# Scaling a PSUM tile by halves, third product one pair later instead of two, first loads on a second queue: pairwise bilinear products on one core

## Chip, cores, metric

One core of a Trainium2 chip. The time is the device time of one execution in microseconds, a median of several runs. One core runs, so there is no die to compare.

In the lines of the profile PE is TensorE's matmuls, PEld its weight loads, ACT ScalarE, DVE VectorE, POOL GpSimd and SP SyncE, whose queue issues most transfers. A line of a page gives, after the bar, the busy time in us and the mean ns of one instruction, then the idle time of the engine just before and what ended it. PSUM is the memory into which TensorE writes its products.

## The reference, cut to what matters

```python
FIELD_SIZE, EMBED_SIZE = 32, 128                 # batch 1024, 496 pairs i < j
v_i, v_j = inputs[:, I_IDX, :], inputs[:, J_IDX, :]
transformed = jnp.einsum('bpd,ped->bpe', v_i, W)  # one 128x128 matrix a pair
return transformed * v_j                          # (1024, 496, 128), 260 MB of fp32
```

## The kernel before

All but the first 15 pairs split x and W into a high and a low part, so that three products of a faster kind (a matmul starts every 0.23 us, a native fp32 one every 0.43) are precise enough for the output check. A pair's PSUM tile is 128 partitions by 1024 fp32, two banks (the prediction says from where), and PSUM holds four such tiles. For each pair:

```python
# F: first product, high*high and low*low, two halves of the batch each
for t in (0, 1):
    for h in range(0, BT, HB):                    # HB = 512, one bank
        nc.tensor.matmul(po[q][:, h : h + HB], w_s[c][t][:, r], x_s[i][t][:, h : h + HB],
                         start=t == 0, stop=t == 1)
nc.scalar.mul(po[q], po[q], 1.0 + EPS)            # A: the whole tile, in place
...
if q >= LAG:                                      # LAG = 2
    if q - LAG >= nq0:
        second(q - LAG)                           # S: third product, two matmuls into the same tile
    finish(q - LAG)                               # D: times x_j on VectorE, then store 512 KB
```

[...] Weights come in chunks of four pairs; ScalarE and GpSimd split each chunk two chunks ahead. What builds the instruction lists from the program (called the compiler here) is free to reorder the instructions of an engine; F, A, S and D are used as names below, with F0, F1, A0, A1 for the half of the batch.

Of the kernel before, what the change touches and what calls it, by code (L numbers as in the profile page):

```python
# [1 line left out]

# [4 lines left out]

F32 = mybir.dt.float32
F32R = mybir.dt.float32r
ALU = mybir.AluOpType  # L10

P = 128
NF = 32
NQ = NF * (NF - 1) // 2
BT = 1024
HB = 512
WC = 4
EPS = 2.0**-12
NATIVE = 5
LAG = 2  # L20


def _pairs():

    return [(i, j) for i in range(NF - 2, -1, -1) for j in range(i + 1, NF)]


@with_exitstack
def kernel(
    ctx: ExitStack,  # L30
    tc: tile.TileContext,
    xt: bass.AP,
    wt: bass.AP,
    out: bass.AP,
):
















    nc = tc.nc
    pairs = _pairs()
    nchunk = NQ // WC

    xpool = ctx.enter_context(tc.tile_pool(name="x", bufs=1))
    spool = ctx.enter_context(tc.tile_pool(name="xs", bufs=2))
    rpool = ctx.enter_context(tc.tile_pool(name="wr", bufs=4))
    wpool = ctx.enter_context(tc.tile_pool(name="ws", bufs=3))
    tpool = ctx.enter_context(tc.tile_pool(name="tmp", bufs=2))  # L60
    opool = ctx.enter_context(tc.tile_pool(name="o", bufs=6))
    ppool = ctx.enter_context(tc.tile_pool(name="ps", bufs=4, space=bass.MemoryType.PSUM))

    x_sb = {}

    def load_x(f, pieces=1):
        x_sb[f] = xpool.tile([P, BT], F32, tag=f"x{f}", name=f"x_{f}")
        s = BT // pieces
        for k in range(pieces):
            nc.sync.dma_start(out=x_sb[f][:, k * s : (k + 1) * s], in_=xt[:, f, k * s : (k + 1) * s])  # L70

    w_raw = {}

    def load_w(c, splits=(0, WC)):
        w_raw[c] = rpool.tile([P, WC, P], F32, tag="w", name=f"w_{c}")
        for a, b in zip(splits, splits[1:]):
            nc.sync.dma_start(out=w_raw[c][:, a:b, :], in_=wt[:, c * WC + a : c * WC + b, :])

    w_s = {}

    def split_w(c):

        raw = w_raw[c].rearrange("p q e -> p (q e)")
        h, l, d = [wpool.tile([P, WC * P], F32R, tag=t, name=f"{t}_{c}") for t in ("wh", "wl", "wd")]
        hs = tpool.tile([P, WC * P], F32, tag="t", name=f"whs_{c}")
        nc.scalar.mul(h, raw, 1.0 - 2.0**-13)  # L86
        nc.gpsimd.tensor_tensor(l, raw, h.bitcast(F32), ALU.subtract)  # L87
        nc.gpsimd.tensor_scalar(hs, h.bitcast(F32), EPS, 1.0, ALU.mult, ALU.mult)  # L88
        nc.gpsimd.tensor_tensor(d, l.bitcast(F32), hs, ALU.subtract)  # L89
        w_s[c] = (h, l, d)  # L90

    x_s = {}

    def split_x(f):

        h, l, d = [spool.tile([P, BT], F32R, tag=t, name=f"{t}_{f}") for t in ("xh", "xl", "xd")]
        for a in range(0, BT, HB):
            s = slice(a, a + HB)
            ls = tpool.tile([P, HB], F32, tag="t", name=f"xls_{f}_{a}")
            nc.scalar.mul(h[:, s], x_sb[f][:, s], 1.0 - 2.0**-13)  # L100
            nc.gpsimd.tensor_tensor(ls, x_sb[f][:, s], h[:, s].bitcast(F32), ALU.subtract)  # L101
            nc.gpsimd.tensor_scalar(l[:, s], ls, 1.0 / EPS, 1.0, ALU.mult, ALU.mult)  # L102
            nc.gpsimd.tensor_tensor(d[:, s], h[:, s].bitcast(F32), l[:, s].bitcast(F32), ALU.subtract)  # L103
        x_s[f] = (h, l, d)

    nq0 = NATIVE * (NATIVE + 1) // 2
    c0 = nq0 // WC

    load_w(0, (0, 1, WC))
    load_x(NF - 2, 2)  # L110
    load_x(NF - 1, 2)
    load_x(NF - 3)
    load_w(1)
    for f in (NF - 4, NF - 5):
        load_x(f)
    load_w(2)

    out_v = out.rearrange("q e b -> q e b")
    po = {}

    def finish(q):
        j = pairs[q][1]
        ot = opool.tile([P, BT], F32, tag="ot", name=f"ot_{q}")
        pieces = 2 if q >= NQ - 2 else 1
        s0 = BT // pieces
        for k in range(pieces):
            s = slice(k * s0, (k + 1) * s0)
            nc.vector.tensor_tensor(ot[:, s], po[q][:, s], x_sb[j][:, s], ALU.mult)  # L128
            nc.sync.dma_start(out=out_v[q, :, s], in_=ot[:, s])

    def second(q):
        i, _ = pairs[q]
        r = slice(q % WC * P, (q % WC + 1) * P)
        for h in range(0, BT, HB):
            nc.tensor.matmul(  # L135
                po[q][:, h : h + HB], w_s[q // WC][2][:, r], x_s[i][2][:, h : h + HB], start=False, stop=True,
                skip_group_check=True,
            )

    for q in range(NQ + LAG):  # L140
        if q < NQ:
            i, j = pairs[q]
            c = q // WC
            if q % WC == 0:
                if c + 3 < nchunk:
                    load_w(c + 3)
                for k in ([c + 2] if c > 0 else [0, 1, 2]):
                    if c0 <= k < nchunk:
                        split_w(k)
            if j == i + 1:  # L150
                for f in ([i - 4] if i < NF - 2 else [NF - 6]):
                    if f >= 0:
                        load_x(f)
                if 0 <= i - 1 < NF - 1 - NATIVE:
                    split_x(i - 1)
            po[q] = ppool.tile([P, BT], F32, tag="po", name=f"po_{q}")
            if q < nq0:
                for h in range(0, BT, HB):
                    nc.tensor.matmul(  # L159
                        po[q][:, h : h + HB],  # L160
                        w_raw[c][:, q % WC, :],
                        x_sb[i][:, h : h + HB],
                        start=True,
                        stop=True,
                    )
            else:
                r = slice(q % WC * P, (q % WC + 1) * P)
                for t in (0, 1):
                    for h in range(0, BT, HB):
                        nc.tensor.matmul(  # L170
                            po[q][:, h : h + HB],
                            w_s[c][t][:, r],
                            x_s[i][t][:, h : h + HB],
                            start=t == 0,
                            stop=t == 1,
                        )
                nc.scalar.mul(po[q], po[q], 1.0 + EPS)  # L177
        if q >= LAG:
            if q - LAG >= nq0:
                second(q - LAG)  # L180
            finish(q - LAG)


# [25 lines left out]
```

## Time and profile before

| of the kernel before | |
|---|---|
| time, median | 898 us |
| span of the profiled run | 896.0 us |
| pace of the split pairs | 1.776 us a pair (from one S to the next, mean) |
| TensorE's own pace, six matmuls | 1.39 us |
| DMA queue, share of 16 engines | 92.3% |
| S with one other F between it and its own F | 356 of 481 |
| S right behind its own F | 125 of 481 |

The pace is well over what any engine needs for a pair; the difference is waiting. The last two rows say how the compiler ordered TensorE, counted from the start times in the trace. The lines themselves stand in the prediction.

### The profile page before, as it was taken

The page shows a single profiled execution, that of the slowest core. Times are in us where ns is not written, and L with a number is a line of the kernel's source. Part 1 is how long each engine was busy: PE and PEld are TensorE (multiplying, and loading weights), DVE is VectorE, ACT ScalarE, POOL GpSimd, SP SyncE. Part 2 cuts the span into 40 slices and gives each one's busy share as a digit, 9 for nine tenths or more (in the row PEclk, how much of TensorE's full clock was granted, in tenths as well). Part 3 has the DMA queues.
Part 4 walks back from the last instruction along what each step waited for, and adds up shares of the span by engine and source line. Part 5 has one row for each costly group of instructions (what it writes and reads, how often), then busy time and mean ns, then how long its engine had stood idle before and what let it go on. Part 6 is the DMA issues. An engine that isn't in the chain of part 4 may idle for free.

```text
span 896.0 us, 10407 instructions
## 1 busy us (share of the span) xinstructions
PE 761.1 (85%) x2946; PEld 526.2 (59%) x2946; DVE 607.0 (68%) x498; ACT 558.2 (62%) x655; POOL 549.5 (61%) x523
## 2 busy tenths in 40 slices
PE   7988888888888888888888888888888888898887
PEld 2455555555666565555565666655656566665665
DVE  3666666666777666676676767776667777677766
ACT  2266666666676566566665667665756666666565
POOL 1878877777666774664747565665655647474441
PEclk9999999999999999999999999999999999999999
DMA  8999999899999898998998999998998899999997
GB/s 329 416 340 370 360 355 343 318 361 338 376 357 362 332 370 327 339 361 320 353 343 336 343 363 356 355 352 321 355 341 334 336 339 330 343 345 339 337 342 304
DMA packets 94666, 310.03 MB, mean 346 GB/s; under 512 B 10513, under 2 KB 10769, under 8 KB 94609
## 3 DMA queue, kind: packets, MB, share of 16 engines
q1 hardware_dynamic: 94608, 309.37, 92.3%
q8 instruction: 23, 0.38, 0.2%
q14 instruction: 35, 0.28, 0.1%
HBM read 49.28 MB, written 260.05 MB: 345 GB/s over the span
## 4 chain that ended last, share of the span: by engine, by line
PE 32%; ACT 25%; issue 19%; POOL 11%; DMA 1%; DVE 0%; POOLq 0%; ACTq 0%; DVEq 0%
ACT po L177 20%; PE po L170 17%; PE po L135 14%; ACT wh L86 4%; POOL wl L87 4%; POOL wd L89 4%; POOL whs L88 2%; DMA out_dram<-ot 1%; ACT xh L100 1%; POOL xls L101 1%; DVE ot L128 0%; POOL xl L102 0%; POOLq L87 0%; ACTq L177 0%; POOL xd L103 0%
## 5 line engine op out<-in xcount | busy, mean ns | idle before, releaser
L128 DVE TENSOR_TENSOR ot<-po,x 128x1024 f32<-128x1024 f32 (+1 forms) x498 | 607.0, 1220 | 285.4 <-ACT po L177 141.7
L177 ACT ACTIVATE po<-po 128x1024 f32<-128x1024 f32 x481 | 476.9, 1009 | 298.5 <-PE po L170 298.5
L135 PE MATMUL po<-xd,wd 128*128 128x512 f32 x962 | 325.7, 420 | 123.8 <-ACT po L177 123.0
L87 POOL TENSOR_TENSOR wl<-w,wh 128x512 fp32r<-128x512 f32 x121 | 154.5, 1277 | 301.7 <-ACT wh L86 301.7
L135 PEld LDWEIGHTS po<-xd,wd 128*128 128x128 f32 x962 | 152.7, 188 | 257.5 <-ACT po L177 162.8
L170 PE MATMUL po<-xh,wh 128*128 128x512 f32 x962 | 300.9, 394 | 0.0
L170 PE MATMUL po<-xl,wl 128*128 128x512 f32 x962 | 298.1, 391 | 0.0
L170 PEld LDWEIGHTS po<-xl,wl 128*128 128x128 f32 x962 | 180.6, 188 | 42.2
L170 PEld LDWEIGHTS po<-xh,wh 128*128 128x128 f32 x962 | 180.6, 188 | 42.1 <-issue 0.5
L89 POOL TENSOR_TENSOR wd<-wl,whs 128x512 fp32r<-128x512 f32 x121 | 156.6, 1294 | 7.9
L86 ACT ACTIVATE wh<-w 128x512 fp32r<-128x512 f32 x121 | 75.5, 624 | 19.3 <-DMA w<-in_wt_dram 19.3
L88 POOL TENSOR_SCALAR whs<-wh 128x512 f32<-128x512 f32 x121 | 75.1, 621 | 10.2
L101 POOL TENSOR_TENSOR xls<-x,xh 128x512 f32<-128x512 f32 x52 | 67.4, 1296 | 4.2
L103 POOL TENSOR_TENSOR xd<-xh,xl 128x512 fp32r<-128x512 f32 x52 | 66.9, 1287 | 2.2
L100 ACT ACTIVATE xh<-x 128x512 fp32r<-128x512 f32 x52 | 32.1, 621 | 13.6 <-PE po L170 8.7
L102 POOL TENSOR_SCALAR xl<-xls 128x512 fp32r<-128x512 f32 x52 | 32.4, 623 | 4.4
L159 PE MATMUL po<-x,w 128*128 128x512 f32 x60 | 29.6, 656 | 6.2 <-DMA x<-in_xt_dram 6.2
L159 PEld LDWEIGHTS po<-x,w 128*128 128x128 f32 x60 | 12.3, 209 | 22.6 <-issue 21.6
L86 ACT ACT_TABLE_LOAD x1 | 1.3, 1283 | 0.7 <-PEq L196 0.7
L196 POOL MEMSET const-float32-0.0<- 128x1 f32 x1 | 0.1, 99 | 0.2 <-issue 0.2
L196 POOL MEMSET const-bfloat16-1.0<- 128x1 bf16 x1 | 0.1, 102 | 0.0
L196 POOL MEMSET const-uint8-127<- 128x1 uint8 x1 | 0.1, 102 | 0.0
(1 smaller groups left out, 0.1 us busy)
## 6 DMA issues: line engine op xcount, KB each, us to landing
out_dram<-ot SPq DMA_DIRECT2D x494, 512.0 KB, 3.8
w<-in_wt_dram SPq DMA_DIRECT2D x123, 256.0 KB, 3.9
x<-in_xt_dram SPq DMA_DIRECT2D x30, 512.0 KB, 6.0
x<-in_xt_dram SPq DMA_DIRECT2D x4, 256.0 KB, 4.4
out_dram<-ot SPq DMA_DIRECT2D x4, 256.0 KB, 2.6
w<-in_wt_dram SPq DMA_DIRECT2D x1, 192.0 KB, 2.6
w<-in_wt_dram SPq DMA_DIRECT2D x1, 64.0 KB, 1.8
```

The costliest lines, as they stand in the source:

```text
L86: nc.scalar.mul(h, raw, 1.0 - 2.0**-13)
L87: nc.gpsimd.tensor_tensor(l, raw, h.bitcast(F32), ALU.subtract)
L88: nc.gpsimd.tensor_scalar(hs, h.bitcast(F32), EPS, 1.0, ALU.mult, ALU.mult)
L89: nc.gpsimd.tensor_tensor(d, l.bitcast(F32), hs, ALU.subtract)
L100: nc.scalar.mul(h[:, s], x_sb[f][:, s], 1.0 - 2.0**-13)
L101: nc.gpsimd.tensor_tensor(ls, x_sb[f][:, s], h[:, s].bitcast(F32), ALU.subtract)
L103: nc.gpsimd.tensor_tensor(d[:, s], h[:, s].bitcast(F32), l[:, s].bitcast(F32), ALU.subtract)
L128: nc.vector.tensor_tensor(ot[:, s], po[q][:, s], x_sb[j][:, s], ALU.mult)
L135: nc.tensor.matmul(po[q][:, h : h + HB], w_s[q // WC][2][:, r], x_s[i][2][:, h : h + HB], start=False, stop=True, skip_group_check=True,)
L159: nc.tensor.matmul(po[q][:, h : h + HB], w_raw[c][:, q % WC, :], x_sb[i][:, h : h + HB], start=True, stop=True,)
L170: nc.tensor.matmul(po[q][:, h : h + HB], w_s[c][t][:, r], x_s[i][t][:, h : h + HB], start=t == 0, stop=t == 1,)
L177: nc.scalar.mul(po[q], po[q], 1.0 + EPS)
```

## The change

The intent: let A start after two of the four matmuls by working half by half, bring S close to its F, and save issue time at the start.

```diff
-LAG = 2
+LAG = 1
@@ (load_x takes the issuing engine)
-    load_x(NF - 2, 2)
-    load_x(NF - 1, 2)
+    load_x(NF - 2, 2, nc.scalar)
+    load_x(NF - 1, 2, nc.scalar)
@@ F and A
-                for t in (0, 1):
-                    for h in range(0, BT, HB):
+                for h in range(0, BT, HB):
+                    for t in (0, 1):
                         nc.tensor.matmul(
                             po[q][:, h : h + HB],
 [...]
-                nc.scalar.mul(po[q], po[q], 1.0 + EPS)
+                    nc.scalar.mul(po[q][:, h : h + HB], po[q][:, h : h + HB], 1.0 + EPS)
```

(A view of the output that did nothing was removed too.)

More of the change, by code (lines that the diff above doesn't have):

```diff
@@ L64, with load_x @@
     x_sb = {}
-    def load_x(f, pieces=1):
+    def load_x(f, pieces=1, eng=None):
         x_sb[f] = xpool.tile([P, BT], F32, tag=f"x{f}", name=f"x_{f}")
@@ L69, in load_x @@
         for k in range(pieces):
-            nc.sync.dma_start(out=x_sb[f][:, k * s : (k + 1) * s], in_=xt[:, f, k * s : (k + 1) * s])
+            (eng or nc.sync).dma_start(out=x_sb[f][:, k * s : (k + 1) * s], in_=xt[:, f, k * s : (k + 1) * s])
     w_raw = {}
@@ L116 @@
     load_w(2)
-    out_v = out.rearrange("q e b -> q e b")
     po = {}
@@ L128, in finish @@
             nc.vector.tensor_tensor(ot[:, s], po[q][:, s], x_sb[j][:, s], ALU.mult)
-            nc.sync.dma_start(out=out_v[q, :, s], in_=ot[:, s])
+            nc.sync.dma_start(out=out[q, :, s], in_=ot[:, s])
     def second(q):
```

## The prediction

> **What bounds the kernel now.** I read the page first (busy shares, then the idle column of the groups), then the table of stretches, then the waits, the timeline of one period, the chain of waits and last the tail. Short names: F is the first four matmuls of a pair (high and low halves, line 170), A is the activation that multiplies the pair's PSUM tile by 1+EPS (line 177), S is the third product (two matmuls, line 135), D is the VectorE multiply by the second field.
>
> ```profile
> PE 761.1 (85%) x2946; PEld 526.2 (59%) x2946; DVE 607.0 (68%) x498; ACT 558.2 (62%) x655; POOL 549.5 (61%) x523
> q1 hardware_dynamic: 94608, 309.37, 92.3%
> L177 ACT ACTIVATE po<-po 128x1024 f32<-128x1024 f32 x481 | 476.9, 1009 | 298.5 <-PE po L170 298.5
> L135 PE MATMUL po<-xd,wd 128*128 128x512 f32 x962 | 325.7, 420 | 123.8 <-ACT po L177 123.0
> L86 ACT ACTIVATE wh<-w 128x512 fp32r<-128x512 f32 x121 | 75.5, 624 | 19.3 <-DMA w<-in_wt_dram 19.3
> ```
>
> No compute engine is full. TensorE's 85% overstates it, because pipelined matmuls overlap in that count. What stands out is a pair that wait for each other: A waits 298.5 us for F, and S waits 123.0 us for A. That is a latency loop, not an engine at its limit. The other suspect is the DMA queue, whose packets fill 92.3% of 16 engines.
>
> One period of the steady state, TensorE alone (start, duration, what, idle before; the second half of the last two F is left out):
>
> ```profile
> 873.59 0.70 PE L135 MATMUL po<-xd,wd 128*128 128x512 f32 x2 [0.26 <-ACT po L177]
> 874.12 0.63 PE L170 MATMUL po<-xh,wh 128*128 128x512 f32 x2
> 874.59 0.62 PE L170 MATMUL po<-xl,wl 128*128 128x512 f32 x2
> 875.05 0.62 PE L135 MATMUL po<-xd,wd 128*128 128x512 f32 x2
> 875.51 0.63 PE L170 MATMUL po<-xh,wh 128*128 128x512 f32 x2
> 875.98 0.62 PE L170 MATMUL po<-xl,wl 128*128 128x512 f32 x2
> 876.43 0.63 PE L135 MATMUL po<-xd,wd 128*128 128x512 f32 x2
> 877.76 0.73 PE L135 MATMUL po<-xd,wd 128*128 128x512 f32 x2 [0.69 <-ACT po L177]
> 878.33 0.63 PE L170 MATMUL po<-xh,wh 128*128 128x512 f32 x2
> ...
> 879.26 0.62 PE L170 MATMUL po<-xh,wh 128*128 128x512 f32 x2
> ...
> 880.61 0.70 PE L135 MATMUL po<-xd,wd 128*128 128x512 f32 x2 [0.26 <-ACT po L177]
> ```
>
> The period is 880.61 - 873.59 = 7.02 us for four pairs (one weight chunk), 1.755 us a pair. A matmul starts every 0.233 us, so six take about 1.39 and four pairs 5.55. The missing 1.47 us lies at two places: an S that follows another S with nothing between (877.76), and an S after two F (880.61). The emitted order is thus not the program's order with LAG 2: never do three F stand ahead of an S. Counting over the trace, 356 of the 481 S have one other F between them and their own, and 125 have none, nearly always the last pair of a chunk. There the chain of waits shows why it is costly:
>
> ```profile
> 876.17 0.48 ACT wh L86
> 876.65 0.04 issue
> 876.69 1.03 ACT po L177
> 877.72 0.04 issue
> 877.76 0.73 PE po L135 x2
> ```
>
> The weight split (0.48 to 0.62 us on ScalarE) delays A, A is 1.0 us long and starts only when the whole F is done, and S waits for the whole A.
>
> In the tail, after the last weight split, S starts stand at 883.45 and 884.84: 1.39 us a pair, TensorE's own pace, even with today's A. So the loop is what holds the middle back.
>
> **What the Trainium skill says.** "ScalarE: Activation LUTs", What ACT_TABLE_LOAD costs: an activation with immediate scale and bias takes 186 ns + 0.833 ns an element, and neighbours overlap by 93 ns. Here 512 elements take 624 ns (612 by the formula) and 1024 in PSUM 1009 (1039): it agrees within 3%. "PSUM — Partial Sum Buffer", Specifications: a bank is 512 fp32 values a partition, so the tile is two banks and each half of the batch is a bank of its own; its section on bank collisions asks for guards by bank. The whole A straddles both, which is why it can't start after two matmuls. "DMA: Bandwidth & Descriptors", Issuing engines are not separate DMA queues: two issuers share the same 16 engines and only issue time is saved. The trace of before has one queue only and can't test it. "Perfetto Trace Analysis", Identifying the Most-Contended Engine, warns that matmul occupancy misjudges headroom; the tail's 1.39 us a pair against 1.755 agrees.
>
> **The change part by part.**
> 1. Scaling by halves with the matmuls reordered (half outside, term inside). Matmul count and weight loads stay (each of the four already has its own load). A becomes two of about 1009 - 512 x 0.833 = 582 ns, overlapping by 93: some 0.98 us of ScalarE a pair against 0.92. Cost 0.06 to 0.12 us x 481 = 30 to 60 us of ScalarE time, 1164 ns against 1009 in the busy column (+75 us), off the path: per chunk 4 x 0.98 + 0.53 + about 0.2 for the field split = 4.7 us, below TensorE's 5.55.
> Gain: the first half of A starts after two matmuls, not four. Today from F's start to its S there are 0.93 + 0.19 + 1.02 + 0.04 = 2.18 us. By halves the first half ends at 0.47 + 0.19 + 0.58 = 1.24, the second at about 1.72. So an S with nothing between stalls TensorE 1.28 - 0.93 = 0.35 us for the first half and about 0.25 more for the second, instead of 1.2; an S behind one F (2.32 us after its own F began, in strict alternation) has 0.6 us in hand, enough to swallow one weight split of 0.52.
> 2. LAG 1. It asks for the alternation F, S of the previous pair, which the order mostly has already. It removes nothing by itself; it takes the tendency to put two F together away. PSUM stays four tiles; in alternation a tile is used about 4.4 us and comes round after 5.55, so no wait for D appears.
> 3. First fields over the ScalarE queue. The first five field pieces cost 2.32 us of issue on the sync queue; x_30 can start about 0.9 us earlier, but x_29 and the next weights then share the engines with it. Native pairs end at 35.2 us now; I count 1 us gain, give or take 1.
>
> Sum for compute: a chunk of 5.55 plus 0.6 for one S without an F between = 6.2 us at most, 1.55 us a pair.
>
> **The DMA floor.** This is what will take over.
>
> ```profile
> 200.00:300.00 100.00, 85.36 (x340) 60.15 (x339) 69.47 (x57) 66.81 (x79) 68.91 (x65) 1.00 0.96 357
> ...
> 600.00:700.00 100.00, 84.86 (x337) 59.74 (x336) 68.40 (x57) 63.66 (x74) 60.55 (x58) 1.00 0.91 341
> 700.00:800.00 100.00, 86.95 (x347) 61.42 (x345) 70.72 (x59) 65.47 (x77) 58.63 (x57) 1.00 0.91 339
> ```
>
> The last two columns are DMA share and GB/s. From 200 to 800 us the share averages 0.925 and D's busy time over 1.22 us gives some 340 pairs, 1.766 us each. So a pair costs 1.766 x 0.925 = 1.63 us of all 16 engines, above the 1.55 of compute. Over the whole run: 92.3% of 896 is 827 us. In the stretch from 20 to 50 us the share reads 1.02 at 408 GB/s, so the engines can be filled. I take 97.5% filling, 1.63 / 0.975 = 1.675 us a pair, because reads of w among the writes will still make holes.
> Span: 34.2 to the end of the native pairs + 481 x 1.675 + 4 of tail = 844, and the measured times lie 2 above the span: **846 us**, 5.8% less.
>
> **Rivals.**
> (a) Order gone wrong: since each half is ready earlier, the compiler may place S right behind its own F always. Then F's start to the end of S is about 2.0 us a pair and the kernel is slower, about 1000 us. For it: it does so already in 125 of 481 places. Against: it does so where the next F has no PSUM tile yet. A milder form, the first half of S behind its own F and the second behind the next, costs 1.39 + 0.12 and stays under the DMA floor.
> (b) Only part of the loop gone: one stall of 0.6 a chunk stays and coincides with a hole in the DMA, so both add up: 6.2 + 0.7 = 6.9 us a chunk, 1.72 a pair, about 868 us.
> (c) DMA packets stretch less than I count. In quiet stretches a 4 KiB packet takes 159 ns, and the 827 us include those at 300 around the weight reads. If writes and reads interleave better, 1.55 to 1.6 a pair and 800 to 815 us.
> (d) ScalarE becomes the bound, by 75 us more of busy time: 633 of 845, 75%, no.
>
> **Range and chances.** The middle is the DMA floor with a little loss; the upper end is (b) with more order noise, the lower (c). 846, range 815 to 880. Faster by over 2% means under 880: 0.86. Within 2%: 0.10, if the order keeps most stalls. Slower: 0.04, rival (a).
>
> **What would show it.** S's wait for A falls from 123 us to under 50; A's group has 962 entries near 580 ns; PE starts alternate F and S at 1.5 to 1.7 us; the DMA share rises to 0.96 or more, D or SP start to wait for landings, and out's time from issue to landing grows from 3.8 us. It is wrong if the share stays at 0.92 with S waiting for A as before, or if S stand directly behind their own F throughout.

## The result, and the profile after

The changed kernel takes **1087.11 us** (median of 4 runs, 1086.47 to 1089.12) against 897.93. The ratio is 1.211 (95% interval 1.209 to 1.213).

The page of the changed kernel, the lines that answer to those of before (A is line 176 now, S 134, F 169):

```profile
PE 858.1 (79%) x2946; PEld 483.7 (44%) x2946; DVE 606.3 (56%) x498; ACT 616.2 (57%) x1136; POOL 548.3 (50%) x523
q1 hardware_dynamic: 94032, 308.32, 75.3%
L176 ACT ACTIVATE po<-po 128x512 f32<-128x512 f32 x962 | 524.6, 580 | 431.5 <-PE po L169 431.2
L134 PE MATMUL po<-xd,wd 128*128 128x512 f32 x962 | 356.5, 444 | 175.2 <-ACT po L176 174.9
L169 PE MATMUL po<-xh,wh 128*128 128x512 f32 x962 | 398.0, 414 | 45.4 <-ACT po L176 44.8
```

Every engine is less busy as a share, the DMA queue most of all (75.3% after 92.3%). The waits between F, A and S grew. The last line is new in kind: F, the pair's *first* product, now waits for ScalarE, 44.8 us, and its weight loads another 154.0 (list of waits). Before it never waited for A (0.0 us before both groups of line 170). What should F have to wait for in A? One period answers (all engines; start, duration, what, idle before):

```profile
603.86 0.39 PE L169 MATMUL po<-xh,wh 128*128 128x512 f32 x1
...
604.09 0.40 PE L169 MATMUL po<-xl,wl 128*128 128x512 f32 x1
604.12 1.07 ACT L176 ACTIVATE po<-po 128x512 f32<-128x512 f32 x2 [0.87 <-PE po L169]
...
604.75 0.73 PE L134 MATMUL po<-xd,wd 128*128 128x512 f32 x2 [0.27 <-ACT po L176]
...
605.24 0.19 PEld L169 LDWEIGHTS po<-xh,wh 128*128 128x128 f32 x1 [0.19 <-ACT po L176]
605.32 0.42 PE L169 MATMUL po<-xh,wh 128*128 128x512 f32 x1
```

603.86 and 604.09 are F0 of a pair; the two activations from 604.12 are A1 of the pair before and A0 of this pair, done at 605.19; then S of the pair before; and only at 605.24 come the weights of F1 of this pair, released by ScalarE. The compiled list of instructions says the same. An excerpt (TensorE, with the engine whose semaphore each instruction waits on; the words at the right are mine):

```
744 L134 Matmult po_2116<-xd_1684,wd_1982 128x512 [waits Activation]     S of the pair before
745 L134 Matmult po_2116<-xd_1684,wd_1982 128x512
746 L169 Matmult po_2128<-xh_1682,wh_1980 128x512 [waits Activation]     F1 of this pair
747 L169 Matmult po_2128<-xl_1683,wl_1981 128x512
748 L169 Matmult po_2140<-xh_1682,wh_1980 128x512 [waits DVE]            F0 of the next pair
749 L169 Matmult po_2140<-xl_1683,wl_1981 128x512
750 L134 Matmult po_2128<-xd_1684,wd_1982 128x512 [waits Activation]     S of this pair
```

(Numbers after the underscore name tiles.) F1 waits on ScalarE although it writes another bank than A0: the dependency is kept for the tile, not for its halves, and in the program A0 stands before F1. The same holds for S: its first matmul writes only the half that A0 scales, yet it waits for A1. Followed to the instruction that is waited for, the list has A0 of the same tile before F1, and A1 of the same tile before S, in all 481 pairs. The chain of waits of the changed kernel shows the loop that this makes:

```profile
604.12 0.59 ACT po L176
604.71 0.04 issue
604.75 0.73 PE po L134 x2
605.48 0.50 PE po L169 x2
...
606.07 0.59 ACT po L176
```

A1, then S of the same pair, then F1 of the next pair, then its A1: 1.95 us a pair, nothing beside it. The A0 that S's first half needs was done at 603.24, and S started at 604.75, right behind A1. F1 is held by two things that end within about 0.1 us of each other here, A0 (605.19) and the S that stands in front of it on TensorE; the chain goes through S. So this loop is the waits inside the tile together with the place of S between F0 and F1, and only the runs with a pinned order, below, tell the two apart. From F0's start of a pair (601.91, for the pair whose S starts at 604.75) to its S there are 2.84 us, against 2.18 in the kernel before and 1.28 in my prediction. From one S to the next a pair takes 2.180 us in the mean, where it was 1.776. In 393 of the 481 places half an F of the next pair lies between F and S, in 75 nothing.

One stretch, to be set beside the same stretch of the kernel before in the prediction:

```profile
600.00:700.00 100.00, 79.16 (x279) 45.18 (x277) 56.72 (x47) 58.03 (x108) 48.81 (x46) 1.00 0.77 288
```

279 matmuls in 100 us where there were 337; the DMA share falls from 0.91 to 0.77 because it has less to do.

### The profile page after: what moved, and what is told of

The parts are those of the page before. It is cut to its first block, busy times and chain, and to the rows that moved or that the text cites. A ratio compares the mean times of both kernels' runs of the same rounds, so it can differ in the third digit from the quotient of the medians.

```text
span 1087.1 us, 11362 instructions
## 1 busy us (share of the span) xinstructions
PE 858.1 (79%) x2946; PEld 483.7 (44%) x2946; DVE 606.3 (56%) x498; ACT 616.2 (57%) x1136; POOL 548.3 (50%) x523
## 3 DMA queue, kind: packets, MB, share of 16 engines
q1 hardware_dynamic: 94032, 308.32, 75.3%
## 4 chain that ended last, share of the span: by engine, by line
PE 57%; ACT 31%; issue 7%; POOL 2%; DMA 1%; ACTq 1%; DVE 1%; DVEq 0%; POOLq 0%
ACT po L176 30%; PE po L134 29%; PE po L169 27%; ACT xh L100 1%; PE po L158 1%; ACTq L176 1%; DMA w<-in_wt_dram 1%; DVE ot L127 1%; POOL xd L103 0%; POOL xls L101 0%; POOL wl L87 0%; ACT wh L86 0%; DMA x<-in_xt_dram 0%; POOL whs L88 0%; POOL xl L102 0%
## 5 line engine op out<-in xcount | busy, mean ns | idle before, releaser
L176 ACT ACTIVATE po<-po 128x512 f32<-128x512 f32 x962 | 524.6, 580 | 431.5 <-PE po L169 431.2
L134 PE MATMUL po<-xd,wd 128*128 128x512 f32 x962 | 356.5, 444 | 175.2 <-ACT po L176 174.9
L169 PE MATMUL po<-xh,wh 128*128 128x512 f32 x962 | 398.0, 414 | 45.4 <-ACT po L176 44.8
L169 PE MATMUL po<-xl,wl 128*128 128x512 f32 x962 | 379.3, 395 | 0.0
L134 PEld LDWEIGHTS po<-xd,wd 128*128 128x128 f32 x962 | 148.1, 188 | 378.2 <-ACT po L176 263.7
L169 PEld LDWEIGHTS po<-xh,wh 128*128 128x128 f32 x962 | 180.8, 188 | 179.3 <-ACT po L176 154.0
```

The costliest lines, as they stand in the source:

```text
L134: nc.tensor.matmul(po[q][:, h : h + HB], w_s[q // WC][2][:, r], x_s[i][2][:, h : h + HB], start=False, stop=True, skip_group_check=True,)
L176: nc.scalar.mul(po[q][:, h : h + HB], po[q][:, h : h + HB], 1.0 + EPS)
```

## The experiments

Every run but the last gave a correct result. Times are medians; the kernel before measured 896 to 898 us beside each.

**Which part of the change costs?** Each alone, and the queue. The theories that the expectations number are stated in the first of them, theory 4 where it comes up.

`lag1_only`: kernel before, `-LAG = 2` / `+LAG = 1`.

> The kernel before with LAG 1 instead of 2 and nothing else. Theory 1 (the loss is a wait inside one PSUM tile: the second half's matmuls F1 wait for the first half's activation A0 of the same tile) expects about the time of before, 880 to 910 us, since A is whole and there is no half to wait for. Theory 2 (LAG 1 puts the third product S too close behind its own first product) expects most of the loss here: 1000 us or more. Theory 3 (the doubled number of activations and their fixed cost) expects 898.

901.83 us, ratio 1.005 (1.002 to 1.008). The order on TensorE stays what it was: 354 S with one other F between, 127 with none. LAG 1 is not the cause.

`halves_only`: kernel before with only the F and A part of the diff.

> The kernel before, LAG 2 and one queue, with only the matmuls reordered by halves and A cut in two, as in the change. Theory 1 expects the whole loss here: 1070 to 1100 us, with F waiting for A some hundred times. Theory 2 expects no loss, 850 to 900 us. Theory 3 expects the loss here too, so it is told from theory 1 by the next run.

1083.13 us, ratio 1.2075 (1.204 to 1.211): all but 4 us of the loss, with LAG 2 and one queue.

`queue_only`: kernel before with only `+ nc.scalar` at the first field loads.

> The kernel before with only the four first field pieces issued on ScalarE's queue. All theories expect 898 within 4 us: some 1 us gained or lost before the native pairs.

894.77 us, ratio 0.9966 (0.9952 to 0.9980): 3 us gained, small but clear of noise. The start of its timeline:

```profile
0.73 1.85 ACTq L70 DMA_DIRECT2D x<-in_xt_dram  x4
...
3.87 12.45 PE L159 MATMUL po<-x,w 128*128 128x512 f32 x22 [3.87 <-DMA x<-in_xt_dram]
```

The field loads go out at 0.73 us instead of 1.65, the first matmul starts at 3.87 instead of 4.56, and the trace shows no gap in the first 22 matmuls, where the kernel before paused after four.

**Is it the wait of F1 for A0, or the halves themselves?**

`acts_last`: the changed kernel, activations written after all four matmuls.

```diff
                 for h in range(0, BT, HB):
                     for t in (0, 1):
                         nc.tensor.matmul(...)
+                for h in range(0, BT, HB):
                     nc.scalar.mul(po[q][:, h : h + HB], po[q][:, h : h + HB], 1.0 + EPS)
```

> The changed kernel with one edit: the two half activations are written after all four matmuls of the pair, so no matmul stands behind an activation of its own tile. The number and size of all instructions is that of the changed kernel. Theory 1 expects nearly all of the loss gone: 890 to 950 us (somewhat over before, since A0 and A1 one after the other end 0.15 to 0.2 us later than one whole A and this lies in the path about twice a chunk, 121 chunks). Theory 2 and theory 3 expect it to stay near 1087 us.

937.49 us, ratio 1.045 (1.042 to 1.048). The same instructions in number and size, LAG 1, and 150 us of the 189 lost are gone, so theories 2 and 3 are out as the main cause. In the compiled list 3 matmuls of F wait on ScalarE, all in the first pairs, where the changed kernel has 483.

`two_tiles`: the changed kernel with a PSUM tile per half.

```diff
-            po[q] = ppool.tile([P, BT], F32, tag="po", name=f"po_{q}")
+            po[q] = [ppool.tile([P, HB], F32, tag=f"po{g}", name=f"po{g}_{q}") for g in (0, 1)]
@@ finish
+        for k in (0, 1):       # D in two instructions of 512 columns, one store
```

> The changed kernel with a PSUM tile per half (512 columns, one bank, four of each half) in place of one tile of two banks; the multiply by the second field is then two instructions of 512 columns, about 0.69 us each. Theory 1 expects the wait of F for A to be gone and the gain that the halves were meant to bring to appear: 830 to 880 us, at a DMA share of 0.93 to 0.98. Theory 2 expects about 1087, since LAG is 1 here. Theory 3 expects about 1087 or more.

928.44 us, ratio 1.034 (1.032 to 1.037). F1 no longer waits for A0, and the result is right, so the chip doesn't need that wait: it came from the tile being one. But the gain I expected did not appear (928 against 830 to 880). The list of waits of this run shows where it went (waiting engine and line, releaser, us, times, longest):

```profile
PEld po L135 <- ACT po L177: 269.6, 700, 0.9
```

With the halves independent, the compiler put nearly every S (478 of 481) before the whole next F had been issued, its first half right behind F1 of its own pair, so the weight loads of S wait for A 700 times a little (195 times, 162.8 us, in the kernel before). My theory of the wait was right but not all: the order on TensorE is a second cause, and I took it to be at work in the kernel before as well, which the next runs test.

**The order on TensorE.** The pin used from here on keeps the instruction order only and adds no wait on the chip (TensorE's compiled list has 1236 semaphore waits in the kernel before and as many in the first run below):

```diff
-                        nc.tensor.matmul(            # F
+                        last[0] = nc.tensor.matmul(
@@
-                second(q - LAG)
+                with tc.issue_after(last[0].ins) if q < NQ else ExitStack():
+                    second(q - LAG)
```

`before_order`: kernel before, LAG 1, this pin.

> The kernel before with LAG 1 and whole activations, and the third product S of a pair pinned, in TensorE's issue order only, behind the first product F of the next pair (no semaphore is added). Theory 4 (what is left of the loop in the kernel before is the order on TensorE, S placed right behind its own F in 125 of 481 places and two F together elsewhere) expects the stalls to shrink to the one weight split a chunk, TensorE near 1.5 us a pair, and the DMA floor of 1.63 us a pair to take over: 845 us, 825 to 870. Its rival, that the order doesn't matter since A or the DMA hold the pace anyway, expects 890 to 905.

**781.54 us**, ratio 0.871 (0.869 to 0.872), better than my range. 480 of 481 S have just one other F between. Page and timeline of this run (A is line 178, S 136, F 171):

```profile
PE 732.3 (94%) x2946; PEld 526.8 (68%) x2946; DVE 606.7 (78%) x498; ACT 567.4 (73%) x655; POOL 550.4 (71%) x523
q1 hardware_dynamic: 94608, 309.37, 100.6%
L136 PE MATMUL po<-xd,wd 128*128 128x512 f32 x962 | 309.0, 402 | 3.3 <-ACT po L178 3.1
```

```profile
500.80 0.63 PE L136 MATMUL po<-xd,wd 128*128 128x512 f32 x2
501.27 0.62 PE L171 MATMUL po<-xh,wh 128*128 128x512 f32 x2
501.73 0.63 PE L171 MATMUL po<-xl,wl 128*128 128x512 f32 x2
502.19 0.62 PE L136 MATMUL po<-xd,wd 128*128 128x512 f32 x2
```

S, F, S, F at 1.39 us, and S waits for A 3.1 us in the whole run, where it was 123.0. The same work, one line of order: 902 (`lag1_only`) to 782 us.

`two_tiles_order`: `two_tiles` with the pin.

> A PSUM tile per half as in the earlier run, with S of a pair pinned behind the whole F of the next pair. The earlier run gave 928 us with its S halves one half product behind their own F. Theory 4 expects 845 us, 825 to 870, as TensorE and VectorE (two multiplies of 0.69 us) then both have about 1.4 us of work a pair. If instead the halves cost in themselves (more instructions, more semaphores), it stays over 900.

779.90 us, ratio 0.869 (0.867 to 0.871), again below my range: the halves on their own tiles cost nothing once the order is right, and gain nothing over whole activations either. (This kernel has the second queue too; the one with whole activations and that queue, at the end of this part, takes 778.4.)

`after_order`: the changed kernel with the pin.

> The changed kernel with the same pin of S behind the next pair's F, one PSUM tile of two banks as in the change. Theory 1 (F1 waits for A0 of its own tile) expects no cure: from F0's start to A0's end 1.24 us, then 0.04, F1 0.46, S 0.46, so about 2.2 us a pair and 1098 us, 1050 to 1120. If the order alone were what cost the changed kernel its time, 840 to 900.

1028.02 us, ratio 1.145 (1.143 to 1.147), 59 us better than unpinned and below my range: the pin left the compiler free to pull F0 of the pair after next forward, and it did so for 187 S. The wait stands plainly in TensorE's timeline:

```profile
600.82 0.39 PE L170 MATMUL po<-xh,wh 128*128 128x512 f32 x1
601.05 0.39 PE L170 MATMUL po<-xl,wl 128*128 128x512 f32 x1
602.11 0.50 PE L170 MATMUL po<-xh,wh 128*128 128x512 f32 x1 [0.67 <-ACT po L177]
```

F0 at 600.82 and 601.05, then F1 only at 602.11, when A0 (601.48 to 602.06 in the same run) is done.

`acts_last_order`: `acts_last` with the pin; it differs from `after_order` only in where the two activations stand.

> The changed kernel, one PSUM tile of two banks and two half activations, with S pinned behind the next pair's F, and the two activations written after all four matmuls. It differs from the pinned changed kernel (1028 us) only in where the two activations stand, so the difference is what the wait of F1 for A0 costs under a fixed order. Theory 1 expects 780 to 800 us: the two A end at 0.93 + 0.19 + 1.20 = 2.32 us after F began, S is due at 2.32, and the DMA sets 1.55 us a pair. If the halves themselves cost, it stays over 900.

814.57 us, ratio 0.908 (0.906 to 0.909). So under the pin the place of two activations is worth 213 us. It is 15 us over my range. A1 waits on A0 of its tile in the compiled list, so the two do not overlap:

```profile
499.92 1.20 ACT L178 ACTIVATE po<-po 128x512 f32<-128x512 f32 x2 [0.67 <-PE po L170]
```

1.20 us against 1.01 for one whole A. S is due 2.32 us after F began, just when the second activation ends, which leaves nothing in hand, and behind a weight split it waits (42.2 us in all for the matmuls, 137.8 for their weight loads). With a tile per half and the pin this cost is gone (779.9).

`before_order_lag2`: as `before_order`, LAG 2, so the order is that of the program before.

> The kernel before with LAG 2 and S pinned behind the F of two pairs later, which is what its program said. It tells what the LAG is worth where the order is kept. With four PSUM tiles, D of a pair (0.2 + 1.22 us) must end within the 1.39 us from its S to the F four pairs on, so TensorE waits a little for D in every pair: about 1.5 to 1.6 us a pair, 785 to 815 us. If it were 780 as with LAG 1, the LAG makes no difference; if near 898, the pin does not help by itself.

779.58 us, ratio 0.869 (0.867 to 0.870): no worse than LAG 1. I expected 5 to 35 us more from D holding PSUM tiles; at 1.52 us a pair there was time for it. So LAG is worth nothing either way, once the order is kept.

`before_order_queue`: `before_order` plus the second queue for the first fields.

> The kernel before with LAG 1, whole activations, S pinned behind the next pair's F, and the first field pieces on ScalarE's queue: the two parts that helped, together. If the gains add up, 3 us less than the pinned kernel: 778 us. If the DMA, full from start to end there, hides the earlier start, 781.

**778.43 us**, ratio 0.867 (0.866 to 0.869): 3 us under `before_order`, as much as the queue gave alone. That the gains add up is likely and not shown: the two ran in different rounds, and `before_order_lag2`, in the same rounds as this one and without the queue, is only 1 us slower. It takes 13.3% less time than the kernel before and its result is correct.

**What bounds the pinned kernels?**

`half_store`: `before_order` that stores half of each result (a wrong result).

```diff
-            nc.sync.dma_start(out=out_v[q, :, s], in_=ot[:, s])
+            nc.sync.dma_start(out=out_v[q, :, :HB], in_=ot[:, :HB])    # but the last two pairs
```

> The pinned kernel before (781.5 us), with only the first half of the batch of each result stored, save the last two pairs: a wrong result on purpose, 126 MB fewer to write. If the DMA queue is what sets 1.51 us a pair in the pinned kernels, as the three of them that meet at 778 to 782 us suggest, the time falls to TensorE's pace: 35 us of native pairs, 481 x 1.39, 4 of tail, 708 us, with some of the weight-split stalls left 705 to 740. If something else sets it, it stays at 770 or more.

747.02 us, ratio 0.833 (0.831 to 0.836): the DMA does hold the pinned kernels, but only 35 us over the next limit. Its stretches:

```profile
100.00:200.00 100.00, 95.91 (x396) 70.31 (x396) 78.89 (x67) 79.60 (x94) 85.04 (x81) 1.00 0.87 304
400.00:600.00 200.00, 200.00 (x835) 149.65 (x835) 169.19 (x139) 162.87 (x184) 145.02 (x137) 1.00 0.68 233
```

From 200 us on TensorE is full, 835 matmuls in 200 us or 1.44 us a pair, not 1.39. From 100 to 200 us it issues only 396 in 100 us while GpSimd is busy 85 of 100, and from 40 to 100 us only 215 in 60 us, with GpSimd busy 57. I read that as GpSimd's field splits, which are dense there. No run tests it, but the list of waits from 33 to 200 us shows a chain that fits: TensorE's weight loads wait for D (11.1 us, at most 4.5 at once), D waits for stores to land (14.4 us, at most 5.4), and on SyncE's queue weight loads, with stores behind them, wait for GpSimd to be done with a buffer (41.9 us, at most 8.1). Both put the result above my range.

All together, medians in us:

| activations | order left to the compiler | S pinned behind the next F |
|---|---|---|
| whole, LAG 1 | 901.8 | 781.5 |
| halves, A0 written before F1 (the change) | 1087.1 | 1028.0 |
| halves, written after F1 | 937.5 | 814.6 |
| halves, a PSUM tile each | 928.4 | 779.9 |

Down a column one sees the wait inside the tile, across a row the order. The left column mixes them, since the order that the compiler chose differs from row to row; how the changed kernel's 189 us divide between wait and order without the pin is not measured. The rows of halves have the second queue, the first row has not; it is worth some 3 us.

## Why the prediction was wrong

1. **The step that failed** is in part 1, the gain: "By halves the first half ends at 0.47 + 0.19 + 0.58 = 1.24, the second at about 1.72." The working took F1 to run on while A0 works, from the remark that "each half of the batch is a bank of its own". In the program as built F1 waits for A0, because both touch one tile. The same working let the first half of S go at 1.28, behind A0 alone; as built it waits for A1. And that the whole A "straddles both" banks was not why it could not start after two matmuls: in the order of before neither half is complete then. What was to end at 1.72 us ended just before S at 2.84. Moving the two activations behind F1 gave back 150 of 189 us, with another order on TensorE, and 213 of 246 under the pin (1028.0 to 814.6, over 781.5). The hint was in my own argument: it said that A by halves could start early *because* of banks, and nothing in the trace of before showed two engines on two halves of one PSUM tile.
2. **The cost side of part 1 was right**: a half activation took 580 ns (582 predicted), and ScalarE at 57% is no bound. The overlap by 93 ns holds between tiles (two in 1.07 us), not within one (1.20 us).
3. **Part 2 was right in its main point**: LAG 1 "removes nothing by itself"; 1.005 alone. That it "takes the tendency to put two F together away" was wrong: the order didn't change (354 and 127 against 356 and 125).
4. **Part 3 had its sign right and its size small**: 3 us instead of 1.
5. **Rival (a)** named a slower kernel of about 1000 us, and 0.04 was far too little for it. Its picture, S behind its own F, was not the main one (75 of 481), and the larger part of the loss stayed when the order was pinned (1028.0, still 130 over the kernel before). That its figure comes near 1087 is luck. Its milder form, S's first half behind its own F and the second behind the next F0, was put at 1.39 + 0.12 us a pair. `two_tiles` has that order in 347 of 481 pairs, and a pair took 1.85 us there in the mean.
6. **The DMA floor was mis-sized.** "A pair costs 1.63 us of all 16 engines" took the share as capacity used. The pinned kernel moves the same bytes at 1.51 us a pair; its packets' time adds up to 100.6% of 778.7, 783 us, not 827. Packets take longer in the starved kernel (one of 4 KiB 171 ns in the mean, against 163 in the pinned one), as rival (c) said. This did not matter for the changed kernel, which never came near.
7. **Of the signs it named**, 962 activations near 580 ns came; S's wait for A rose from 123.0 to 174.9 us instead of falling under 50, and the DMA share of the stretch fell from 0.91 to 0.77.
8. **That the loop was "what holds the middle back" was right**, and the tail's 1.39 us a pair was the proof that more was to be had; the pin, not the halves, got it.

## What to carry to other kernels

Before you cut an operation in two so that the halves overlap, ask at what grain the program keeps its dependencies: two halves of one tile, written and read by turns, can become a tighter chain than the whole was; give each half a tile of its own, or write both readers after both writers. Look at the order that was built, not at the order that was written: count on TensorE how many other products stand between a product and its consumer, and pin it where the count is wrong. A high DMA share in a kernel with gaps is not a floor.

## What the Trainium skill lacked or had wrong

- "PSUM — Partial Sum Buffer", PSUM bank collisions: its rule is to guard by bank. It does not say that a program may guard a tile of two banks as one; here that made F1 wait for A0 of the other bank, and S's first half for A1 (1028.0 us against 814.6 with the activations moved, and 779.9 with a tile per bank, all pinned).
- No page that I read says that the built order on TensorE may differ from the program's, nor how to hold it: LAG 2 was emitted with at most one other F ahead of S, and the pin was worth 902 to 782 us.
- "ScalarE: Activation LUTs", What ACT_TABLE_LOAD costs: its overlap of 93 ns between neighbours held for activations on different tiles (two in 1.07 us) and not where the second waits for the first on the same tile (1.20 us). Its formula is 30 ns over what PSUM to PSUM took here (1009 and 580 ns against 1039 and 612).
- "Perfetto Trace Analysis", Identifying the Most-Contended Engine, warns that occupancy of the 16 DMA engines misleads. This is no gap: it was right, and I built my floor on that occupancy all the same. The same bytes took 827 us of packet time in the kernel before and 783 in the pinned one.
